# An order planner that looks 3.5 channel tiles ahead instead of 2.5, and fills 0.9 of TensorE's pauses instead of 0.8

## The chip, the cores and the metric

The kernel runs on one core of a Trainium2 chip. A time is the device time of one execution in microseconds (us). One core has TensorE (PE in the profile, with PEld for its weight loads), VectorE (DVE), ScalarE (ACT), GpSimd (POOL) and SyncE (SP, which here only issues DMAs). Each engine runs its own instructions in the order in which the program holds them, and waits on semaphores for the others.

## What is computed

The input x is (2, 48, 48, 768) in float32: two sequences of 2304 tokens with 768 channels. Two layers follow each other, both with a group norm ahead and a residual add behind:

```python
x = x + _L0_conv_ref(_gn(x), w_qkv, w_out)      # 7x7 neighbourhood attention, 12 heads of 64
x = x + _L1_conv_ref(_gn(x), in_proj_w, ...)    # a bidirectional selective scan
```

The second layer is the longer one. It projects the tokens to 1536 inner channels x and as many gates z, and for each direction (forwards with one set of weights, backwards with another):

```python
x = silu(dwconv(x))                              # depthwise, 4 taps
dt, B, C = split(x_proj_w @ x)                   # 48, 16 and 16 rows
delta = softplus(dt_proj_w @ dt + dt_proj_b)
h[t] = exp(delta[t] * A) * h[t-1] + (delta[t] * x[t]) * B[t]     # 16 states for each channel
y[t] = sum over states (h[t] * C[t]) + x[t] * D
```

The result is `out_proj_w @ ((y_forward + y_backward) * silu(z))`.

## The kernel before

**Units.** The scans are cut into 288 units: 2 sequences, 2 directions, 6 chunks of 384 tokens, 12 tiles of 128 channels. `scan` (L1180) writes down one unit, which has number x. It has four groups of four states (`group`, L1211), and each group has these steps:

- the fill of an `hb` tile with delta * x * B, 128 x 1544 (`first`, L1225), on DVE or on POOL; the plan may choose for three of the four groups (`alt`)
- four exponentials on ACT into a `da` tile in PSUM (L1247); there are two `da` tiles, and each holds what one scan instruction takes
- two scan instructions on DVE (L1258), each for two states
- the product with C on POOL (L1273), and a copy of the last state on ACT (L1281)
- twelve transposes on PE that add the group's products into `py` (`add_up`, L1290)

There are seven `hb` tiles; one is free again when its `add_up` is done. Behind the four groups ACT copies `py` to `yt` (L1316). Forwards it goes to memory; backwards PE turns back and adds both directions (L1343), DVE multiplies by the gate (L1353), and the result goes to memory. For three units at a time `deltas_of` (L1128) loads x, makes the products for delta on PE (L1151), the softplus on ACT (L1162, with a table load before and behind it) and delta * x on POOL (L1175).

**Jobs.** All else is work beside the scans: the projections of attention with its scores, softmax and outputs (`attention`, L529), the projection to x and z with the convolution taps on DVE (`in_proj`, L880; taps at L935), the projection to dt, B and C (`x_proj`, L1048) and the output projection (`out_proj`, L1057). Matrix products go through `product` (L372, matmuls at L382), three matmuls to a piece. For sequence 0, attention stands alone ahead of the scans; for sequence 1 it stands beside the scans of sequence 0.

**The plan.** Nothing of this is issued at once. Every piece of work is added to an `Order` (L91) with its engine, an estimated duration, the cells that it reads and writes, and a key. The key is a due time counted in units: 17.25 means a quarter into unit 17. Work flagged `job` fills in; all other work is a main. `Order.run` (L153) then walks through a model of the five engines and sets the order:

- `mains` holds the keys of the mains that are not placed yet. The lowest is `mains[-1]`. Only work with a key up to `horizon`, which is that key plus `LOOK` (L170), may be placed. If nothing can be placed, the horizon is moved by 1 until something can.
- For each engine it takes the piece with the best rank: the earliest start first, where all that could start within 150 ns count as equal, and then the lowest key. `early` lowers the key in this comparison: by 20 for delta's steps, by 4 for `add_up`.
- A piece waits where its buffer tag is still full (`BUFS`, L314: 5 for weights `w`, 7 for `hb`, 2 for `u`, `dlt` and `uz`, 2 for the PSUM banks `mm`).
- A piece ahead of the lowest main that would hold up an exponential is set back by half of that (L193).

Where the model sees PE without work for over 800 ns inside a unit, it puts idle transposes there (`idle`, L1487): matmuls on the identity that go to unused columns of `py` (L1491). Their number is a share of the pause less 300 ns, divided by 109 ns.

```python
gap = t - free["PE"]
if e == "PE" and spare and gap > self.GAP:
    y = Work()
    y.eng, y.ns, y.key, y.job, y.size = e, 0.8 * (gap - 300.0), x.key, True, 0
```

The order that comes out is the program. The estimated durations set nothing but this order.

Of the kernel before, what the change touches and what calls it, by code (L numbers as in the profile page):

```python
# [93 lines left out]
class Order:  # L94
# [2 lines left out]


    SEM = 90.0
    LOOK = 2.5  # L100
    DUE = 100.0
    GAP = 800.0
    TAIL = {"PE": 120.0, "ACT": 50.0, "DVE": 45.0, "POOL": 10.0, "SP": 0.0}
# [49 lines left out]
    def run(self):  # L153
        free = dict.fromkeys(self.TAIL, 0.0)
        ready = {e: [] for e in free}
        slots, dma = {}, 0.0
        mains = sorted((x.key for x in self.works if not x.job), reverse=True)
        done_keys = {}
        for x in self.works:
            if not x.waits:  # L160
                ready[x.eng].append(x)
                assert not x.alt
        out = []
        left = len(self.works)
        extra, spare = 0.0, False
        while left:
            while mains and done_keys.get(mains[-1], 0):
                done_keys[mains[-1]] -= 1
                mains.pop()
            horizon = (mains[-1] if mains else 1e9) + self.LOOK + extra  # L170
            best = None
            for e, works in ready.items():
                pick = None
                soon = min((max(free[e], x.ready) for x in works if x.due), default=1e12)
                for x in works:
                    if x.key > horizon:
                        continue
                    t, more = max(free[e], x.ready), {}
                    for b in x.bufs:
                        if not b.end:  # L180
                            had = slots.get((b.pool, b.tag), ())
                            n = more[b.tag] = more.get(b.tag, 0) + 1
                            if len(had) + n > b.bufs:
                                old = had[n - 1 - b.bufs]
                                if old.left:
                                    t = None
                                    break
                                t = max(t, old.end + self.SEM)
                    if t is None:
                        continue  # L190
                    over = 0.0
                    if mains and x.key > mains[-1] < self.last and not x.due:
                        over = max(0.0, t + x.ns - soon - self.DUE) / 2  # L193
                    rank = (max(t + over, free[e] + 150.0), x.first)
                    if pick is None or rank < pick[0]:
                        pick = rank, t, x
                if pick and (best is None or pick[1] < best[0]):
                    best = pick[1], pick[2], e
            if not best:

                extra += 1.0
                assert extra < 400, "the plan is stuck"
                continue
            extra = 0.0
            t, x, e = best
            ready[x.eng].remove(x)
            gap = t - free["PE"]
            if e == "PE" and spare and gap > self.GAP:
                y = Work()
                y.eng, y.ns, y.key, y.job, y.size = e, 0.8 * (gap - 300.0), x.key, True, 0  # L210
                y.then, y.bufs, y.due, y.fn = [], [], False, lambda y=y: self.idle(y.ns)
                out.append((free[e], y))
            if x.opens is not None:
                spare = x.opens
            if x.alt:
                ready[x.alt[0]].remove(x)
                if e != x.eng:
                    x.eng, x.ns = x.alt
            for b in x.bufs:
                if not b.end:  # L220
                    slots.setdefault((b.pool, b.tag), []).append(b)
            free[x.eng] = t + x.ns
            if x.eng == "SP":
                dma = max(dma, t + 500.0) + x.size / 290.0
                end = max(dma, t + x.ns) + 2100.0
            else:
                end = t + x.ns + x.tail
            for b in x.bufs:
                b.left -= 1
                b.end = max(b.end, end)  # L230
            for y in x.then:
                y.waits -= 1
                y.ready = max(y.ready, end + self.SEM * (y.eng != x.eng))
                if not y.waits:
                    ready[y.eng].append(y)
                    if y.alt:
                        ready[y.alt[0]].append(y)
            if not x.job:
                done_keys[x.key] = done_keys.get(x.key, 0) + 1
            out.append((t, x))  # L240
            left -= 1
        return out
# [1299 lines left out]
```

## Time and profile before

| | |
|---|---|
| median of 4 runs | 7051.0 us (7042.06 to 7054.28) |
| the profiled execution | 7042.06 us, of which 7040.3 us are the span from the first instruction to the last |
| mean granted TensorE clock in it | 0.977 |
| busy in the span | DVE 6062.6 us, PE 6318.4, POOL 5447.4, ACT 4971.3 |
| first scan, end of the last scan | 1053 us, 7003.6 us |
| scan instructions (L1258) | 2304, 1749 ns each |
| idle transposes (L1491) | 4431 in 324 pauses |

Busy time of PE counts a matmul from its start to its modelled end, and overlapping ones once. An arrow `<-` in a wait names what ended it. The clock is the share of full speed that the throttle granted to TensorE. In the lines of waits the three numbers are the total in us, the number of waits, and the longest.

Five stages follow from what stands beside the scans: attention of sequence 0 alone (0 to 1053 us), scans with input projections of sequence 0 (to about 2060 us), scans nearly alone (to 2460 us), scans with the attention of sequence 1 and then the start of its input projections (to 4260 us), and scans with the projections of sequence 1 and all output projections (to the end).

### The profile page before, as it was taken

How to read it: one execution, taken by the hardware profiler on the slowest of the kernel's cores; microseconds unless marked ns; L12 is line 12 of the kernel's file. 1: busy time of each engine (PE TensorE's matmuls, PEld its weight loads, DVE VectorE, ACT ScalarE, POOL GpSimd, SP SyncE). 2: the span in 40 equal slices, each digit the busy share in tenths (PEclk: the TensorE clock that was granted, in tenths of full speed). 3: DMA queues.
4: the chain of work that ended last, by engine and by line, in shares of the span. 5: the costliest groups of instructions: out<-in, count | busy, mean ns of one | idle time of the engine just before them, and what ended most of it. 6: DMA issues, size and time to landing. Idle time of an engine off the chain costs nothing.

```text
span 7040.3 us, 105645 instructions
## 1 busy us (share of the span) xinstructions
PE 6318.4 (90%) x38151; PEld 4831.2 (69%) x38151; DVE 6062.6 (86%) x6217; ACT 4971.3 (71%) x10948; POOL 5447.4 (77%) x1951
## 2 busy tenths in 40 slices
PE   7999989999989998999988888888888898999888
PEld 5666556666666776676666656666678887777777
DVE  2353449999999999998998999999999999999998
ACT  1332248788888788887888778788876667777764
POOL 0000008888989999898898878999999999999997
PEclk9999989999999999999999999999999999999999
DMA  6565454445556444554444354343466676655553
GB/s 190 172 203 173 139 163 126 135 142 153 155 157 197 151 148 140 152 175 148 127 144 133 112 168 135 97 143 113 140 181 189 179 217 194 194 178 156 161 171 104
DMA packets 1337699, 1101.32 MB, mean 156 GB/s; under 512 B 136329, under 2 KB 1327417, under 8 KB 1337145
## 3 DMA queue, kind: packets, MB, share of 16 engines
q1 hardware_dynamic: 1337176, 1094.56, 51.9%
q8 instruction: 303, 4.96, 0.3%
q14 instruction: 220, 1.79, 0.1%
HBM read 881.41 MB, written 213.57 MB: 156 GB/s over the span
## 4 chain that ended last, share of the span: by engine, by line
DVE 39%; PE 18%; ACT 16%; POOL 12%; issue 9%; DMA 5%; SPq 1%; DVEq 0%; POOLq 0%; ACTq 0%
DVE hb L1258 26%; POOL hb L1273 8%; DVE hb L1225 7%; ACT da L1247 5%; PE mm_qk L382 4%; POOL hb L1225 4%; DVE uz_u L935 4%; PE mm_ao L382 2%; PE mm_v L382 2%; PE py L1290 2%; PE mm_xin L382 2%; ACT pr L785 1%; DMA bc<-xdb 1%; ACT pT L832 1%; ACT L1163 1%
## 5 line engine op out<-in xcount | busy, mean ns | idle before, releaser
L1258 DVE TENSOR_TENSOR_SCAN hb<-da,hb 128x772 f32<-128x772 f32 x2304 | 3927.9, 1749 | 179.4 <-ACT da L1247 144.8
L1273 POOL TENSOR_TENSOR hb<-hb,bc 128x1536 f32<-128x1536 f32 x1152 | 3654.0, 3187 | 371.7 <-DVE hb L1258 332.7
L1247 ACT ACTIVATE da<-dlt,A 128x384 f32<-128x384 f32 x4608 | 2677.2, 584 | 916.4 <-DVE hb L1258 845.0
L1290 PE MATMUL py<-ident,hb 128*128 128x128 f32 x13824 | 1747.9, 279 | 267.6 <-POOL hb L1273 260.3
L1290 PEld LDWEIGHTS py<-ident,hb 128*128 128x128 f32 x13824 | 1563.6, 143 | 526.2 <-POOL hb L1273 420.6
L1225 POOL TENSOR_TENSOR hb<-u,bc 128x1544 f32<-128x1544 f32 x495 | 1584.6, 3203 | 22.0 <-PE py L1290 15.3
L1225 DVE TENSOR_TENSOR hb<-du,bc 128x1544 f32<-128x1544 f32 x657 | 1143.4, 1746 | 36.2 <-ACT du L1202 26.2
L1175 POOL TENSOR_TENSOR u<-dlt,u 128x384 f32<-128x384 f32 x288 | 263.8, 918 | 531.8 <-ACT dlt L1162 418.4
L382 PE MATMUL mm_z<-xc,w_z 128*128 128x384 f32 x1728 | 608.7, 492 | 6.9 <-ACT dlt L1157 3.8
L382 PE MATMUL mm_xin<-xc,w_x 128*128 128x390 f32 x1656 | 591.0, 502 | 26.4 <-DVE uz_u L935 16.7
L382 PE MATMUL mm_out<-stage_y,w_o 128*128 128x192 f32 x3168 | 560.5, 332 | 17.9 <-ACT dlt L1157 6.4
L1491 PE MATMUL py<-ident 128*128 128x128 f32 x4431 | 551.2, 277 | 0.0
L382 PEld LDWEIGHTS mm_out<-stage_y,w_o 128*128 128x128 f32 x3168 | 521.5, 193 | 29.4 <-ACT dlt L1157 10.6
L1491 PEld LDWEIGHTS py<-ident 128*128 128x128 f32 x4431 | 504.6, 143 | 28.8 <-issue 25.9
L901 POOL MEMSET xc<- 128x18 f32 x4 | 0.5, 123 | 633.8 <-DVE sm L779 633.8
L382 PEld LDWEIGHTS mm_xin<-xc,w_x 128*128 128x128 f32 x1656 | 310.5, 195 | 239.2 <-issue 36.2
L935 DVE SCALAR_TENSOR_TENSOR uz_u<-mm_xin,conv_w,uz_u 128x384 f32<-128x384 f32 x792 | 428.7, 610 | 49.9 <-ACT uz_u L928 47.7
L382 PE MATMUL mm_qk<-xc_xn,w_qk 128*128 128x384 f32 x1296 | 458.6, 500 | 14.3 <-DVE ev L601 2.6
L382 PEld LDWEIGHTS mm_z<-xc,w_z 128*128 128x128 f32 x1728 | 314.4, 192 | 193.4 <-issue 8.8
L382 PEld LDWEIGHTS mm_qk<-xc_xn,w_qk 128*128 128x128 f32 x1296 | 240.4, 194 | 173.7 <-issue 21.0
L785 ACT ACTIVATE pr<-pr,sm 128x308 f32<-128x308 f32 x432 | 234.5, 544 | 126.1 <-DVE sm L779 126.0
L1306 PE MATMUL py<-ident,vt 128*128 128x128 f32 x864 | 155.4, 290 | 150.8 <-ACT yt L1316 150.4
(163 smaller groups left out, 6768.5 us busy)
## 6 DMA issues: line engine op xcount, KB each, us to landing
w_o<-in_w_opT SPq DMA_DIRECT2D x264, 384.0 KB
bc<-xdf SPq DMA_DIRECT2D x96, 768.0 KB
bc<-xdb SPq DMA_DIRECT2D x96, 768.0 KB
w_qk<-in_w_qkv SPq DMA_DIRECT2D x144, 384.0 KB
w_x<-in_w_inT SPq DMA_DIRECT2D x144, 384.0 KB
w_z<-in_w_inT SPq DMA_DIRECT2D x144, 384.0 KB
w_ao<-in_w_out SPq DMA_DIRECT2D x72, 384.0 KB
u<-uf SPq DMA_DIRECT2D x48, 576.0 KB
```

Of the source, the lines that this page charges most:

```text
L382: nc.tensor.matmul(acc[:m, o0 : o0 + cl], wb[:, wi, wo : wo + m], xb[:, xi, xo : xo + cl], start=c == 0, stop=c == n - 1,)
L785: nc.scalar.activation(pr[j].ap, pr[j].ap, AF.Exp, bias=sm[:, j : j + 1], scale=-1.0, accum_out=sm[:, 2 + j : 3 + j],)
L832: copy(pT[:nk, ks, j, :], bank(pt, 512 - P)[:nk, ks.start * P : ks.stop * P].rearrange("p (k q) -> p k q", q=P),)
L935: nc.vector.scalar_tensor_tensor(u, px[:, at[j] : at[j] + cl], q["conv_w"][:, k, j : j + 1], u, ALU.mult, ALU.add,)
L1175: lambda j=j: nc.gpsimd.tensor_mul(u[:, j, h], dl[:, j, c], u[:, j, h]), at + 0.06 + 0.25 * j,
L1225: on.tensor_mul(cells(hb, SG), by.unsqueeze(1).to_broadcast([P, SG, W]), bc[g].ap)
L1247: lambda: nc.scalar.activation(cells(da, 2)[:, j % 2, h], dl[:, jd, c], AF.Exp, scale=q["A"][:, k, i : i + 1]),
L1258: lambda: nc.vector.tensor_tensor_scan(flip(hb[at2]), flip(da[:, : 2 * W]), flip(hb[at2]), 0.0, ALU.mult, ALU.add),
L1273: lambda: nc.gpsimd.tensor_mul(cells(hb, SG)[:, :, h], cells(hb, SG)[:, :, h], bc[NSG + g][:, :, c]),
L1290: nc.tensor.matmul(py[:tp, t * P : (t + 1) * P], cells(hb, SG)[:, j, h][:, tb[t]], ident, start=False, stop=g == NSG - 1 and j == SG - 1 a ...
L1306: nc.tensor.matmul(py[:tp, t * P : (t + 1) * P], vt[:, tb[t]], ident, start=t == 0, stop=False, is_transpose=True, skip_group_check=True,)
L1491: nc.tensor.matmul(marks["py"][:, CL : CL + P], ident, ident, start=False, stop=False, is_transpose=True, skip_group_check=True,)
```

## The change

```diff
-    LOOK = 2.5
+    LOOK = 3.5
```

```diff
             if e == "PE" and spare and gap > self.GAP:
                 y = Work()
-                y.eng, y.ns, y.key, y.job, y.size = e, 0.8 * (gap - 300.0), x.key, True, 0
+                y.eng, y.ns, y.key, y.job, y.size = e, 0.9 * (gap - 300.0), x.key, True, 0
```

The first edit lets work be placed whose key is up to 3.5 units past the lowest unplaced main. The second makes the idle transposes of a pause take up 0.9 of the pause less 300 ns. All instructions but the idle transposes are the same ones as before; what moves is their order on every engine, and for some fills (L1225) whether DVE or POOL does them.

## The prediction, made before the changed kernel ran

> **What bounds the kernel now.** I read the page first: busy shares and slices.
>
> ```profile
> PE 6318.4 (90%) x38151; PEld 4831.2 (69%) x38151; DVE 6062.6 (86%) x6217; ACT 4971.3 (71%) x10948; POOL 5447.4 (77%) x1951
> ...
> PE   7999989999989998999988888888888898999888
> ...
> DVE  2353449999999999998998999999999999999998
> ```
>
> PE looks busiest over the whole span, but the slices part it: in the first six (to 1053 us) PE is full and DVE at 0.2 to 0.5, then DVE is at 0.9 to the end. PE's later busy time also holds the idle transposes. The chain of work that ended last agrees:
>
> ```profile
> DVE 39%; PE 18%; ACT 16%; POOL 12%; issue 9%; DMA 5%; SPq 1%; DVEq 0%; POOLq 0%; ACTq 0%
> ```
>
> DVE leads, but with ACT, PE and POOL between: DVE stops for each of them. The busy time by stage says how much it stops.
>
> ```profile
> 0.00:1060.00 1060.00, 971.24 (x5063) 640.67 (x5064) 426.26 (x1512) 315.95 (x849) 13.33 (x17) 0.97 0.58 174
> 1060.00:2060.00 1000.00, 910.49 (x4810) 656.15 (x4809) 927.68 (x794) 819.23 (x1565) 876.66 (x314) 0.97 0.47 143
> 2060.00:2460.00 400.00, 370.75 (x2189) 284.06 (x2188) 386.48 (x240) 310.66 (x669) 382.89 (x138) 0.99 0.60 177
> 2460.00:4260.00 1800.00, 1616.98 (x10506) 1202.62 (x10505) 1657.67 (x1716) 1469.25 (x3620) 1559.08 (x554) 0.98 0.48 146
> 4260.00:6660.00 2400.00, 2116.29 (x13406) 1764.79 (x13404) 2329.82 (x1721) 1825.07 (x3782) 2294.21 (x820) 0.98 0.55 163
> 6660.00:7040.00 380.00, 332.63 (x2186) 282.93 (x2185) 334.72 (x240) 231.14 (x466) 321.20 (x113) 0.99 0.46 135
> ```
>
> After the window come PE, PEld, DVE, ACT, POOL, the clock, the DMA share and GB/s. DVE's idle time is 72 us in the second stage, 14 in the third, 142 in the fourth (attention beside scans), 70 in the fifth, 45 at the end: 343 us of 5980. DVE's own work hardly changes, so those 343 us are all that a new order can win from, or add to. The waits of DVE in the fourth stage say on whom:
>
> ```profile
> DVE hb L1258 <- ACT da L1247: 62.2, 54, 5.5
> DVE zs L1353 <- PE mm_yb L1343: 23.4, 10, 4.3
> DVE pr L779 <- PE mm_s L769: 16.3, 10, 5.8
> DVE hb L1225 <- PE py L1290: 8.7, 4, 4.2
> ```
>
> By far the most is the scan that waits for its exponentials; then come waits on PE, 52 us with the smaller ones (2.3 and 1.3 us). The same view gives 69.6 us on ACT and none on PE in the second stage, 11 on ACT in the third, 39 on ACT and 5.6 on PE in the fifth.
>
> **What the change does to the order.** I compared the order of instructions of both programs, engine by engine.
>
> - Until the first scan every engine has the same instructions placed: on PE 432 matmuls for q and k, 432 for v, 216 for attention's output, 72 for x. Attention pieces stand a few places apart; the weights for v are now fetched ahead of most of those for q and k. That load falls into the time in which PE waits for the group norm (28 to 44 us), so I cost it at nothing; bounds -6 and +6 us, the time that 1.18 MB take at the 190 GB/s of the page's first slice.
> - From the last unit's scans to the end the products stand in the same order. The 37 us behind the last scan stay.
> - In between, attention of sequence 1 runs up to 2 to 4 units earlier (608 masked-score instructions placed on DVE at unit 102 instead of 584), and its next input projection is 30 taps ahead at unit 144. In the second stage the jobs are where they were or later (168 taps instead of 180 at unit 12): there the horizon isn't what holds them, but the buffers.
> - DVE gets 659 fills instead of 657, POOL two fewer. PE gets 5127 idle transposes instead of 4431.
>
> **The sum, term by term, against the profiled execution (7042.06 us).**
>
> *Fills.* From the groups:
>
> ```profile
> L1225 POOL TENSOR_TENSOR hb<-u,bc 128x1544 f32<-128x1544 f32 x495 | 1584.6, 3203 | 22.0 <-PE py L1290 15.3
> L1225 DVE TENSOR_TENSOR hb<-du,bc 128x1544 f32<-128x1544 f32 x657 | 1143.4, 1746 | 36.2 <-ACT du L1202 26.2
> ```
>
> Two more on the engine that sets the end: 2 x 1.746 = +3.5 us. POOL's 6.4 us less lie beside.
>
> *Waits on PE.* A job that stands between two `add_up`s holds back the release of `hb` and `py`. I laid the rows of PE's order out with durations from the trace (24 matmuls of 384 columns in 7.94 us, so 0.33 us each; 0.115 for 128 columns, 0.165 for 192, 0.11 for a transpose; idle ones left out), and summed, between each two `add_up`s, what goes over 5 us; seven `hb` tiles cover less. In the fourth stage this falls from 76.9 to 56.3 us, by 27%, and stretches over 10 us go from eight to four. 27% of the 52 us of waits is -14 us. In the second it rises from 1.4 to 6.5 us and in the fifth from 0.3 to 4.2: there waits on PE are 0 and 5.6 us now, so little is known. Bounds 0 and +9 us; I take 0, since the stretches there mostly stay under 6 us.
>
> *Waits on ACT.* A scan waits if ACT's order holds more work between two exponential pairs than DVE's order holds between the scans two apart (two `da` tiles). With the mean durations of the groups, the excess summed over 2304 scans is 745 us before and 730 after; the trace has 215 us of real waits on ACT, so such a sum is only good as a ratio. By stage: second 153.9 to 171.1 (+11% of 69.6 us: +8, of which I take half, as two `da` tiles' lead can hide it), third 42.7 to 35.4 (-17% of 11: -2), fourth 287.5 to 265.4 (-8% of 78: -6), fifth level (0), end 16.9 to 14.9 (-1). Together -5 us; bounds -9 and +8.
>
> *Idle transposes.* 696 more at 109 ns (their pitch in the timeline) are 76 us in 325 pauses, 0.23 us each. After the old ones PE still stood idle for 0.45 us in the median pause, which hides the rest; in 105 pauses under 0.06 us was left, and there the next `add_up` or product starts up to 0.23 us later: at most 105 x 0.23 = +25 us if all were on the path. On the other side the clock: 0.97 to 0.99 in the scan stages. At 1.00, 2% of the some 300 us that PE has on the chain behind the first stage (18% of 7040 less 971) would be -6. I take 0: most of these pauses end at `add_up`, with `hb` tiles in hand.
>
> Do transposes keep the clock up at all? Near the end (6860 to 6990 us) `add_up` and idle transposes are 72 of PE's 112 busy us, and the granted clock there is 1.00, so the row says they do, and the term keeps both its ends. The Trainium skill (TensorE: Matmul & The Clock Gate, Part 4: PE-mode transpose) says the opposite, that transposes don't count as busy for the clock gate; by it the second edit could only cost, and the sum below would lie between itself and 25 us more.
>
> Sum: +3.5 - 14 - 5 + 0 = -15.5, so 7026.5 us for an execution like the profiled one. That was the fastest of the four runs, 9 us under their median, so **7036 us** as a median: -0.2%.
>
> **The rivals.**
>
> *It cancels, or the look binds little.* Against the gain stands that most of DVE's waiting is on the `da` ring, and no horizon widens that:
>
> ```profile
> ACT da L1247 <- DVE hb L1258: 845.0, 1239, 3.8
> ```
>
> ACT stands ready for 845 us and waits for a scan to free a `da` tile: the exponentials are already as far ahead as two tiles let them. The Trainium skill (Perfetto Trace Analysis, Identifying Performance Opportunities) reads a gap that repeats on the engine that should be full as too few buffers for the next tile; by it the look would give nothing, and the sum would be the fills' +3.5 alone, 7054 us in the scale of the median. By the rows: if the fourth stage's relief is halved (-10 instead of -20) and the second stage takes its +8: 3.5 - 10 - 3 + 8 = -1.5, so 7050 us in the scale of the median. Counting anything from 7037 to 7065 (the 0.2% that a measurement of this kernel can tell from no change): 0.26.
>
> *Slower: jobs in front of `add_up`.* A longer look offers PE more jobs whose inputs are there, and each that starts just before an `add_up` is ready holds it. In the order, stretches of over 4 us between `add_up`s rise from 15 to 23 in the second stage, from 33 to 38 in the fourth, from 14 to 19 in the fifth: 18 more. A DVE wait of this kind costs 2.3 us now (23.4 us in 10 waits). If all hit: +42, with the fills and the second stage's ACT waits +53.5, so 7104; if two thirds hit and the fourth stage gains nothing, +28 + 11.5, so 7090. It decides as soon as 13 of the 18 hit while the fourth stage's relief stays: 13 x 2.3 = 30 cancels the 15.5 and the 14 us of the bound. For it: the second and fifth stages have low waits on PE now and only lose. Against it: seven `hb` tiles have covered most stretches under 6 us so far. Chance of slower by over 0.2%: 0.32; likeliest time in that case 7085.
>
> *The forecast*, where the fourth stage's relief holds: 0.42.
>
> **Numbers.** Range: down to 6995, where all 52 us of PE waits in the fourth stage go (38 more than I took, and 3 more on ACT); up to 7100, near the far end of the slower rival. I leave about 0.08 below and 0.1 above.
>
> **What would show it.** Right: first scan at 1053 us within 6; DVE's idle time from 2460 to 4260 us down from 142 to about 122, with fewer waits for mm_yb and mm_s; 659 fills on DVE; idle in the second stage near 72 to 80 us. For the slower rival: waits of L1353, L1079 or L1225 on PE in the second and fifth stages, where there were 5.6 us. For cancelling: 343 us of DVE idle behind the first scan, only elsewhere. Wrong altogether: a DMA wait that neither program's order shows, or a first stage that moves by over 10 us.

## The result, and the profile after

The changed kernel takes 7055.5 us (median of 33 runs, 7040.7 to 7070.46) against 7048.2 us for the kernel before on the same chip (median of 53 runs, 7033.77 to 7070.19). The ratio is 1.001, 95% interval 1.0005 to 1.0015: slower by 0.1%, where 0.2% faster was forecast. The forecast's range holds the time, its sign is wrong.

The profiled execution of after took 7063.15 us (span 7061.4, mean granted clock 0.978), 8 us over its median; that of before took 7042.06, 6 us under its own. Of the 21 us between the two traces only 7 us lie between the medians, which has to be kept in mind below.

The page's busy line of after, and the engines' shares of its chain:

```profile
PE 6400.2 (91%) x38847; PEld 4898.2 (69%) x38847; DVE 6071.5 (86%) x6219; ACT 4977.9 (70%) x10948; POOL 5443.2 (77%) x1949
...
DVE 42%; PE 22%; ACT 16%; issue 9%; POOL 7%; DMA 4%; SPq 0%; DVEq 0%; POOLq 0%; ACTq 0%
```

The two fills that went to DVE are there (6219 instructions instead of 6217), and PE has 696 matmuls and 82 us more. Next the busy times of after by stage, in the same stretches and columns as in the prediction:

```profile
0.00:1060.00 1060.00, 985.34 (x5145) 646.83 (x5146) 439.46 (x1520) 332.05 (x873) 20.32 (x20) 0.98 0.58 174
1060.00:2060.00 1000.00, 909.17 (x4772) 651.25 (x4772) 922.43 (x789) 813.05 (x1559) 887.24 (x316) 0.97 0.48 144
2060.00:2460.00 400.00, 372.41 (x2170) 282.33 (x2168) 388.36 (x246) 313.31 (x675) 375.88 (x136) 0.99 0.57 171
2460.00:4260.00 1800.00, 1621.87 (x10579) 1218.21 (x10578) 1646.19 (x1709) 1452.71 (x3583) 1541.74 (x548) 0.97 0.48 146
4260.00:6660.00 2400.00, 2152.17 (x13824) 1794.71 (x13823) 2314.58 (x1701) 1814.89 (x3754) 2275.71 (x813) 0.98 0.55 160
```

The stretches are fixed in time and the work isn't: in the first, DVE is busy for 13 us more, because the scans begin earlier. So from here on I count the span in parts: the time until the first scan starts, DVE's busy time from there on, and DVE's idle time from there on. Only about 3 us behind the last DVE instruction are left over. The fill alone (first of the experiments below) has before's order but for the idle transposes, so it stands here as a second execution of that order:

| profiled execution | first scan starts, us | DVE busy behind it | DVE idle behind it | span |
|---|---|---|---|---|
| before | 1053.0 | 5641.0 | 343.4 | 7040.3 |
| the fill alone | 1050.3 | 5641.2 | 344.6 | 7039.0 |
| after | 1040.5 | 5649.7 | 367.8 | 7061.4 |
| after less before | -12.5 | +8.7 | +24.4 | +21.1 |

Two effects of opposite sign: the first stage got 12 us shorter (10 against the fill alone), and the scans stop for 24 us more. By stage, second to last, with the stages cut at the same scans in every run, DVE's idle time is 79, 11, 157, 86 and 35 us, where it was 75, 13, 142, 70 and 43 (69, 15, 151, 70 and 40 with the fill alone: a single stage can differ by 8 us between two executions of one order). The fourth stage, for which I had forecast the gain, lost 15 us (6 against the fill alone), and the fifth 16. DVE's waits of after in 2460 to 4260 us (total, number, longest) say where in the fourth:

```profile
DVE hb L1258 <- ACT da L1247: 67.4, 59, 6.2
DVE zs L1353 <- PE mm_yb L1343: 17.4, 9, 5.7
DVE sm L800 <- ACT pr L785: 14.7, 11, 5.2
DVE pr L779 <- PE mm_s L769: 10.6, 7, 5.1
DVE uz_u L935 <- ACT uz_u L928: 10.3, 11, 2.7
DVE xr_x L705 <- PE mm_ao L382: 7.8, 3, 3.8
DVE hb L1225 <- PE py L1290: 6.4, 5, 4.6
```

Waits for `mm_yb` and `mm_s` did fall, from 39.7 to 28.0 us, but `mm_ao` gave some back (1.3 to 7.8). Everything on ACT rose: the scans' exponentials by 5 us, the softmax by 7 (7.8 to 14.7), the taps by 8 (2.7 to 10.3). Together ACT's part is 100 us instead of 78 (81 with the fill alone).

How such a wait looks is shown by the largest new one, in the fifth stage (DVE's idle time in the units from 168 on rose from 5 to 22 us in twelve units, and it did so again in the run with the look alone). From the timeline of after (start, duration, engine, line; in brackets the idle time before and what ended it):

```profile
4766.97 1.28 ACT L961 ACT_TABLE_LOAD   x1
...
4768.27 2.13 ACT L961 ACTIVATE uz_u<-uz_u 128x2304 f32<-128x2304 f32 x1
...
4770.24 5.11 PE L382 MATMUL mm_xin<-xc,w_x 128*128 128x390 f32 x12
4770.41 1.28 ACT L962 ACT_TABLE_LOAD   x1
...
4775.39 1.23 ACT L928 ACTIVATE uz_u<-mm_xin,conv_b,conv_w 128x384 f32<-128x384 f32 x2 [2.50 <-PE mm_xin L382]
4776.52 0.58 ACT L1247 ACTIVATE da<-dlt,A 128x384 f32<-128x384 f32 x1
4776.66 3.24 DVE L935 SCALAR_TENSOR_TENSOR uz_u<-mm_xin,conv_w,uz_u 128x384 f32<-128x384 f32 x6 [6.25 <-ACT uz_u L928]
```

ACT has a SiLU with its two table loads (4.7 us from 4766.97), then a few short copies, then stands for 2.5 us at L928 for the projection's matmuls, and the exponentials of the next scan are queued behind L928. DVE waits 6.25 us at a tap. What ends this wait is PE's product (5.11 us from 4770.24), and L928 directly behind it; the SiLU had ended 3.7 us earlier and isn't on this path. So a wait that the profile puts down to ACT is here in large part one for PE. Nothing in it is a new instruction. It is the same pieces laid in another order, and here a product on PE, its copy on ACT and the tap on DVE fell together.

### The profile page after: what moved, and what is told of

It reads as the page before. It is cut to its first block, busy times and chain, and to the rows that moved or that the text cites. A ratio compares the mean times of both kernels' runs of the same rounds, so it can differ in the third digit from the quotient of the medians.

```text
span 7061.4 us, 107020 instructions
## 1 busy us (share of the span) xinstructions
PE 6400.2 (91%) x38847; PEld 4898.2 (69%) x38847; DVE 6071.5 (86%) x6219; ACT 4977.9 (70%) x10948; POOL 5443.2 (77%) x1949
## 3 DMA queue, kind: packets, MB, share of 16 engines
q1 hardware_dynamic: 1337176, 1094.56, 51.8%
## 4 chain that ended last, share of the span: by engine, by line
DVE 42%; PE 22%; ACT 16%; issue 9%; POOL 7%; DMA 4%; SPq 0%; DVEq 0%; POOLq 0%; ACTq 0%
DVE hb L1258 28%; DVE hb L1225 7%; POOL hb L1273 5%; ACT da L1247 4%; PE mm_qk L382 4%; DVE uz_u L935 4%; PE mm_v L382 2%; PE mm_ao L382 2%; PE py L1290 2%; POOL hb L1225 2%; PE mm_xin L382 2%; PE da L825 1%; ACT uz_u L928 1%; ACT pr L785 1%; PE mm_z L382 1%
## 5 line engine op out<-in xcount | busy, mean ns | idle before, releaser
L1225 POOL TENSOR_TENSOR hb<-u,bc 128x1544 f32<-128x1544 f32 x493 | 1578.7, 3204 | 41.1 <-PE py L1290 30.6
L1225 DVE TENSOR_TENSOR hb<-du,bc 128x1544 f32<-128x1544 f32 x659 | 1146.6, 1747 | 41.8 <-ACT du L1202 29.8
L1491 PE MATMUL py<-ident 128*128 128x128 f32 x5127 | 625.7, 276 | 0.0
L1491 PEld LDWEIGHTS py<-ident 128*128 128x128 f32 x5127 | 577.9, 142 | 32.5 <-issue 29.3
L382 PEld LDWEIGHTS mm_z<-xc,w_z 128*128 128x128 f32 x1728 | 315.9, 192 | 196.9 <-issue 12.5
L1151 PE MATMUL mm_dl<-dt,dtw 49*128 49x384 f32 x576 | 250.3, 538 | 53.3 <-ACT dlt L1157 18.6
```

The source lines that it names most:

```text
L382: nc.tensor.matmul(acc[:m, o0 : o0 + cl], wb[:, wi, wo : wo + m], xb[:, xi, xo : xo + cl], start=c == 0, stop=c == n - 1,)
L1151: lambda j=j, acc=acc: nc.tensor.matmul(acc[:, c], w[:, j * P : (j + 1) * P], dt[:, c], start=True, stop=True),
L1225: on.tensor_mul(cells(hb, SG), by.unsqueeze(1).to_broadcast([P, SG, W]), bc[g].ap)
L1491: nc.tensor.matmul(marks["py"][:, CL : CL + P], ident, ident, start=False, stop=False, is_transpose=True, skip_group_check=True,)
```

## The experiments

Two theories stood against each other. **A: the fill costs nothing, and the look's new order is what moved the time; it is one deal of the pieces among many**, whose stops can't be read from PE's or ACT's order alone. **B: either the fill lengthens PE's work, or looking further ahead has a cost of its own**, with more pieces in front of those that are due. A deal is here any order that the plan lays from the same pieces. The letters in the expectations are each run's own. Each kernel ran beside the kernel before on one chip (7 to 12 executions, 4 of the runs without idle transposes and with late jobs set back), and each ratio is to that one; it can differ by up to 0.05% from the quotient of the two medians. "Idle" is DVE's idle time behind the first scan in the profiled execution; before has 343.4 us.

**The fill alone**

```diff
-                y.eng, y.ns, y.key, y.job, y.size = e, 0.8 * (gap - 300.0), x.key, True, 0
+                y.eng, y.ns, y.key, y.job, y.size = e, 0.9 * (gap - 300.0), x.key, True, 0
```

> The second edit alone: look 2.5, pauses filled to 0.9. The plan's model doesn't count the idle transposes, so every other instruction keeps its place, and only the number of idle transposes rises (about 4431 x 9/8). Theory A (a re-dealt order made the 7 us): level with before, within 4 us, first scan and DVE's idle time unchanged. Theory B (the fill runs over and delays the adds): 5 to 10 us slower, with more waits of DVE on PE. Theory C (a higher clock): 3 to 6 us faster, with a granted clock above 0.977.

Measured: 7046.55 us against 7046.19, ratio 0.9998 (0.9989 to 1.0007). First scan at 1050.3 us, idle 344.6. The order is the one of before but for the idle transposes, and the sum of the stops is the same. A holds: the second edit does nothing that could be told from zero within 0.1%.

**The look alone**

```diff
-    LOOK = 2.5
+    LOOK = 3.5
```

> The first edit alone: look 3.5, pauses filled to 0.8. The order is that of the changed kernel, with fewer idle transposes. Theory A (the re-dealt order makes the difference): 5 to 10 us slower than before, as the whole change. Theory B (the fill makes it): level with before within 4 us.

Measured: 7056.59 us, ratio 1.0015 (1.0006 to 1.0024). First scan at 1039.5, idle 361.6: by stage 75, 9, 160, 83 and 35 us, nearly what after has. From before to here the parts are -13.5, +5.2 and +18.2 us, together +10, which is the ratio. The whole effect of the change is the first edit's.

**No idle transposes at all**

```diff
-                y.eng, y.ns, y.key, y.job, y.size = e, 0.8 * (gap - 300.0), x.key, True, 0
+                y.eng, y.ns, y.key, y.job, y.size = e, 0.0 * (gap - 300.0), x.key, True, 0
```

> Look 2.5 and no idle transposes at all; every other instruction keeps its place. It prices the whole fill. If the fill is free and only holds the clock: a lower granted clock (0.90 or less in the scan stages) and 5 to 40 us more. If the transposes do nothing for the clock: the clock stays at 0.977 and the time stays within 5 us, or falls by up to 25 us where they ran into the adds.

Measured: 7116.61 us, ratio 1.0105 (1.0091 to 1.0119). In the profiled execution (7134.48 us, the longest of the four) the mean granted clock is 0.932 instead of 0.977, the first scan starts at 1061.2, idle is 419.6. Three of its stretches:

```profile
1060.00:2060.00 1000.00, 843.88 (x3930) 580.22 (x3928) 923.01 (x794) 808.57 (x1547) 875.89 (x311) 0.92 0.46 140
...
2460.00:4260.00 1800.00, 1549.21 (x9512) 1141.48 (x9511) 1632.05 (x1683) 1439.43 (x3567) 1539.20 (x546) 0.94 0.46 141
4260.00:6660.00 2400.00, 1963.12 (x11140) 1589.62 (x11138) 2294.41 (x1709) 1805.90 (x3713) 2247.20 (x802) 0.91 0.55 162
```

The clock is the seventh column, 0.91 to 0.94 where before had 0.97 to 0.98. So the idle transposes do hold the clock, and they are worth 1% in all. The clock fell less than expected (0.90 or less), and the time rose more (5 to 40 us). From 0.8 to 0.9 nothing of that is left to win: the clock of the fill alone is 0.980.

**A constant that means nothing: 91 ns instead of 90 for a release in the plan's model**

```diff
-    SEM = 90.0
+    SEM = 91.0
```

> A control: look 2.5, fill 0.8, and the plan's allowance for a semaphore 91 ns in place of 90. It means nothing by itself, but ties fall otherwise and most of the order is dealt anew. Theory A (any new deal moves the time by some 5 to 25 us either way): a difference from before of 5 us or more, of either sign, with DVE's idle time behind the first scan moved by as much. Theory B (only a longer look moves the time): level within 4 us.

Measured: 7055.16 us, ratio 1.0014 (1.0005 to 1.0023); idle 357.7, of it 154 in the fourth stage, where waits on ACT are 103 us. This is a control: 1 ns in a model that only sets the order. It costs as much time as the look does. The fourth stage's idle time alone would not show it (151 with the fill alone), but its waits on ACT do, 103 us against 78 and 81, and after has 100.

**The same constant at 89**

```diff
-    SEM = 90.0
+    SEM = 89.0
```

> A second control: look 2.5, fill 0.8, and 89 ns for a semaphore in the plan in place of 90. Theory A (before is one deal among many, and a lucky one for its neighbours): 0 to 15 us slower, as with 91. If before is an ordinary deal: equally likely faster or slower, by 5 to 15 us.

Measured: 7042.27 us, ratio 0.9991 (0.9982 to 0.9999). Idle is 353.6, 10 us more than before, but this deal leaves 650 fills to DVE instead of 657, and DVE's busy time is 12 us less. The expectation that before is a lucky deal, with 0 to 15 us to lose, missed: this one is some 6 us faster.

**The longer look only while the lowest due time is before -3, that is in the first stage**

```diff
-            horizon = (mains[-1] if mains else 1e9) + self.LOOK + extra
+            look = 3.5 if mains and mains[-1] < -3.0 else self.LOOK
+            horizon = (mains[-1] if mains else 1e9) + look + extra
```

> Look 3.5 only until the lowest unplaced due time reaches -3 (attention of sequence 0), 2.5 behind it, fill 0.8. The order of the scans is nearly that of before. In the runs so far the order with look 3.5 had its first scan at 1040 us and that with 2.5 at 1050 to 1054. Theory A (the first stage wins some 12 us, the scans lose some 20): 8 to 14 us faster than before, first scan at about 1041 us, DVE idle for 343 us behind it as before. Theory B (the early first scan is paid back in the scans, for instance because later work isn't there yet): level with before, and more than 350 us idle behind the first scan.

Measured: 7033.74 us, ratio 0.998 (0.9971 to 0.9989). First scan at 1040.8, idle 348.8; the fourth stage's is 142, as before. The first stage's 12 us can be had alone. This version is the fastest of all, by 0.2% against before; its margin over the 0.14% that a meaningless 1 ns moved is small, and it rests on one deal.

**Late jobs are set back as well.** The model sets a piece back that would hold up an exponential, but not a job that is itself overdue. If such jobs on ACT make the waits, this should take them away:

```diff
-                    if mains and x.key > mains[-1] < self.last and not x.due:
+                    if mains and (x.job or x.key > mains[-1]) and mains[-1] < self.last and not x.due:
```

> Look 2.5, fill 0.8, and the setback of work that would hold up an exponential holds for jobs that are late too, so that six norms no longer stand in a row on ACT. Theory A (DVE waits where ACT holds a long block of job work between exponentials): DVE's waits on ACT fall from 215 us to 190 or less, and the time by 10 to 30 us. Theory B (the blocks are no cause, any deal gives about this): within 10 us of before, waits on ACT at 205 to 225 us.

Measured: 7143.99 us, ratio 1.0134 (1.0121 to 1.0147), idle 459.6. Neither expectation came. The waits of DVE in the fourth stage:

```profile
DVE uz_u L935 <- ACT uz_u L928: 70.6, 16, 15.0
DVE hb L1258 <- ACT da L1247: 47.4, 44, 4.2
DVE pr L779 <- PE mm_s L769: 18.1, 10, 11.7
DVE xr_x L705 <- PE mm_ao L382: 15.7, 7, 3.6
DVE ev L601 <- PE mm_qk L382: 10.9, 4, 6.6
```

The wait aimed at fell (62.2 to 47.4 us), and the one for the jobs themselves rose from 2.7 to 70.6: a tap or a score stands in DVE's order too, and if its input is set back on ACT, DVE stops there instead, with the scans queued behind it. The order that favours the exponentials did not remove the waits on ACT; it moved them.

**Looks of 3.0 and 2.0**

```diff
-    LOOK = 2.5
+    LOOK = 3.0
```

> Look 3.0, fill 0.8. If the length of the look has an effect of its own on the scans, this lies between 2.5 (0) and 3.5 (+10 us): about +5. If each length is just another deal: anywhere from -10 to +20 us, with the first scan somewhere between 1040 and 1054 us.

Measured: 7062.06 us, ratio 1.0015 (1.0006 to 1.0023); first scan 1054.7, idle 367.7.

```diff
-    LOOK = 2.5
+    LOOK = 2.0
```

> Look 2.0, fill 0.8. If the scans' idle time grows with the length of the look, this has less than 343 us of it and is 5 to 15 us faster behind the first scan. If each length is a deal, it has 340 to 380 us. In either case the first scan at 1050 us or later.

Measured: 7072.21 us against 7055.65, ratio 1.0022 (1.0014 to 1.0031); first scan 1050.4, idle 364.7, 660 fills on DVE. A shorter look costs more than the longer one does: time doesn't rise with the look.

**The longer look with the other two deals**

```diff
-    SEM = 90.0
-    LOOK = 2.5
+    SEM = 89.0
+    LOOK = 3.5
```

> Look 3.5, fill 0.8, and 89 ns for a semaphore in the plan in place of 90: the longer look dealt anew. With look 2.5 the deals 90, 89 and 91 gave 343, 354 and 358 us of DVE idle behind the first scan; with 3.5 the deal 90 gave 363 and 370. Theory A (only the deal counts): 340 to 360 us idle here, first scan near 1040 us, 5 to 15 us faster than before. Theory B (the longer look costs the scans some 20 us by itself): 365 us or more, 5 us or more slower than before.

Measured: 7080.31 us, ratio 1.0031 (1.002 to 1.0043); first scan 1040.0, idle 392.9, 184 of it in the fourth stage. Its waits there:

```profile
DVE hb L1258 <- ACT da L1247: 76.4, 64, 6.7
DVE zs L1353 <- PE mm_yb L1343: 19.9, 8, 5.3
DVE hb L1225 <- PE py L1290: 19.3, 7, 10.7
DVE xr_x L705 <- PE mm_ao L382: 18.3, 8, 8.8
DVE pr L779 <- PE mm_s L769: 10.8, 7, 5.1
```

```diff
-    SEM = 90.0
-    LOOK = 2.5
+    SEM = 91.0
+    LOOK = 3.5
```

> Look 3.5, fill 0.8, 91 ns for a semaphore: the same question with another deal. Theory A: 340 to 360 us of DVE idle behind the first scan, 5 to 15 us faster than before. Theory B: 365 us or more, 5 us or more slower.

Measured: 7052.27 us, ratio 0.999 (0.9981 to 0.9999); first scan 1049.3, idle 353.6. By their expectations the deal at 89 ns speaks for a cost of the look itself and the one at 91 ns against it. So one nanosecond up or down makes the longer look's kernel 0.1% faster or 0.3% slower than before. The ratios by look:

| look | model's release 89 ns | 90 ns | 91 ns |
|---|---|---|---|
| 2.0 | | 1.0022 | |
| 2.5 | 0.9991 | 1 (before) | 1.0014 |
| 3.0 | | 1.0015 | |
| 3.5 | 1.0031 | 1.0015 | 0.999 |

At 2.5 the mean is 1.0002, at 3.5 it is 1.0012. Each has a spread of 0.2 to 0.4% over deals that mean nothing, and the neighbours on both sides of 2.5 are slower than it. Before is also the deal with the least idle time behind the first scan of all that ran (343 us; the others have 345 to 460).

**One load of the group norm earlier**

```diff
-            ("SP", 400, fetch, [mv], [gT]),
+            ("SP", 400, fetch, [gs], [gT]),
```

> Look 2.5, fill 0.8; the group norm's second small load (w_gTb) is planned behind the first one instead of behind the statistics, so that on SP's queue it stands ahead of the fetch of xc. The order of the scans changes in a few places only. Theory A (that queue order is the larger part of the first stage's 12 us): PE's wait for w_gTb falls from 4.8 to 1 us or less, the first scan comes at 1044 to 1048 us, 4 to 8 us faster. Theory B (the 12 us come from attention itself): first scan at 1049 us or later, within 3 us of before.

This looks for the 12 us of the first stage. In before's timeline, between attention of sequence 0 and its group norm:

```profile
938.84 0.56 DVE L705 TENSOR_TENSOR xr_x<-mm_ao,xr_x 128x384 f32<-128x384 f32 x1 [2.72 <-PE mm_ao L382]
939.80 0.43 SPq L889 DMA_DIRECT2D xc<-x1T  x1
940.32 0.58 SPq L431 DMA_DIRECT2D w_gTb<-c_gmatT  x1
946.22 2.69 PE L457 MATMUL mm_gnb<-gn_gb,w_gTb 32*128 32x1 f32 x12 [4.81 <-DMA w_gTb<-c_gmatT]
```

and in after's:

```profile
916.37 0.84 SPq L889 DMA_DIRECT2D xc<-x1T  x1
...
935.24 0.38 SPq L431 DMA_DIRECT2D w_gTb<-c_gmatT  x1
937.54 1.47 PE L457 MATMUL mm_gnb<-gn_gb,w_gTb 32*128 32x1 f32 x12 [0.77 <-DMA w_gTb<-c_gmatT]
```

In before the load of the group matrix (96 KB) is issued right behind the fetch of `xc` (1161 KB), on the same DMA queue. By the packets of the trace the fetch's data move from 940.9 to 945.0 us and the load's only from 944.5 on, and PE waits 4.8 us for it. In after the fetch was issued at 916.37, 19 us ahead of the load, and the queue is free of it by then: the load's packets move from 936.3 to 936.9. PE's wait for this load is 0.8 to 1.0 us in all runs with a look of 3.0 or 3.5, and 4.8 to 5.4 us in those that keep 2.5 and the load's old place. With the edit above, which plans the load earlier in every group norm, the wait is gone at a look of 2.5 too, and from the last `mm_ao` to the first scan it takes 108 us instead of 114 (113 with the fill alone; after: 106). But attention ended at 942.0 instead of 938.8 us in this deal, so the first scan came at 1050.1 and not where A had put it. Ratio 0.9988 (0.9979 to 0.9997), idle 361.4, with 653 fills on DVE. So the queue accounts for some 5 of the 12 us. The other part is the end of attention itself, 934.2 in after, and 936.5 to 944.6 in the other deals of looks from 2.0 to 3.0, but for the one with late jobs set back (934.9). It isn't the look's for sure: with 91 ns and a look of 3.5 attention ended at 942.9, and that deal's first scan is at 1049.3.

## Why the prediction was wrong

**The idle transposes: right.** Taken as 0 in bounds of -6 and +25. Alone they gave 0.9998; the 82 us more of PE work lie in PE's pauses, and the clock rose from 0.977 to no more than 0.980. That transposes keep the clock up was read from one stretch; taking them away showed it (0.932 and 1.05%). The sentence of the Trainium skill that was weighed there (TensorE: Matmul & The Clock Gate, Part 4: PE-mode transpose) doesn't hold for these float32 transposes, which are issued as transposes (`is_transpose=True`).

**The fills: right.** 659 instead of 657 on DVE. DVE's busy time behind the first scan grew by 5.2 us with the look alone, 3.9 of them at L1225.

**The first stage: wrong.** Taken as 0 within 6 us, and it moved by 12.5 (13.5 with the look alone). I weighed the early load of v's weights, and compared the places of PE's matmuls, which were the same. What I did not compare were SP's places: a small load that had been queued right behind a fetch of 1161 KB. In after that fetch went out 19 us ahead of the load. By the prediction's own words this was "wrong altogether", and some 5 us of it are the one gain of the look with a known cause.

**The waits on PE: sized too large, by a misread price.** In the fourth stage -14 was forecast and -6.5 came (51.8 to 45.3; -3.3 with the look alone; and 56.8 with the fill alone, so the change is hardly clear of what one order gives twice). The price was half of the true one. The sum took 0.33 us for each matmul of 384 columns that the program has, but 24 matmuls in 7.94 us is a count of the trace's records, and the trace shows two records for each of these products: up to the first scan the program has 432 matmuls for q and k, and the trace 864 (number, then nanoseconds of one, then first and last start in us).

```profile
L382 PE MATMUL mm_qk<-xc_xn,w_qk x432: 486/486/1009, 44.0 to 603.8; 128*128 128x384 f32 x144
...
L382 PE MATMUL mm_qk<-uz_xn,w_qk x432: 486/486/591, 115.3 to 756.2; 128*128 128x384 f32 x144
```

With every record counted, PE's sum for the fourth stage falls from 294 to 276 us, by 6% and not by 27%, which would have made the term -3 us. Stretches over 4 us then rise from 52 to 54 in the second stage, 83 to 87 in the fourth and 87 to 88 in the fifth, 7 and not 18 more. The fifth stage gave back 8 us (4 with the look alone), at the far end of the bound that I gave for the second and the fifth.

**The waits on ACT: the step that failed.** "-6" for the fourth stage came as +22 (77.7 to 100.3; 99.3 with the look alone; 81.3 with the fill alone), and "level" for the fifth as +11 (39.2 to 50.4). Behind the first scan they went from 205 to 239 us in all, +34 (+29 with the look alone), where -5 was forecast. The step took a sum over ACT's order against DVE's order as a ratio of real waits, and did the same for PE. Laid out in the same way for the other orders, the two sums for the fourth stage say nothing of the waits that the trace then has (the columns are the look, and the model's release where it isn't 90 ns; 3.5 is the run with the look alone; the stage is cut at the same scans in all, which for 3.5 gives 263 where the prediction had 265.4; PE's sums are at the prediction's price):

| fourth stage, us | 2.5 (before) | 2.5, 91 | 2.5, 89 | 3.0 | 2.0 | 3.5 | 3.5, 89 | 3.5, 91 |
|---|---|---|---|---|---|---|---|---|
| ACT's sum by the order | 287 | 223 | 285 | 243 | 227 | 263 | 275 | 271 |
| waits on ACT in the trace | 78 | 103 | 84 | 86 | 93 | 99 | 100 | 79 |
| PE's sum by the order | 77 | 68 | 57 | 59 | 64 | 56 | 46 | 71 |
| waits on PE in the trace | 52 | 43 | 51 | 48 | 49 | 48 | 70 | 57 |

The order with the lowest sum for ACT has the longest waits on ACT, and the one with the lowest for PE the longest on PE; over the eight, both pairs rather run against each other. At two records for a product PE's sums are 294, 266, 259, 264, 287, 276, 252 and 285, and 252 still stands with the longest waits. The sum holds each engine against DVE alone, and the stops shown above are made by three: DVE waits for ACT at a tap, ACT waits for PE's product, and the exponentials are queued behind. It also leaves out jobs that DVE itself waits for (softmax and taps, 15 of the 22 us). Why the longer look's orders make ACT stop more stays open. I had one pair of sums and no second order to test them on, and 223 us would have read as a larger gain than the one I forecast.

**The rivals.** Slower by jobs in front of `add_up`: not so. Waits on PE went from 5.6 to 14 us in the fifth stage and stayed under 1 us in the second, against the 13 of 18 waits of 2.3 us that it needed. The rival of cancelling has the right number: 7055.5 lies in its 7037 to 7065. Its reason doesn't fit: the look didn't bind little, it gave 12 us in one place and took 18 to 24 in others. And the 845 us weighed there are ACT's, while the sentence of the Trainium skill cited with them (Perfetto Trace Analysis, Identifying Performance Opportunities) is about the engine that should be full, which here is DVE.

**Shown, and not shown.** Shown: the fill does nothing within 0.1%, the look's order does it all, its two parts have opposite signs, and a change of the plan that means nothing moves the time by about as much in either direction. Only argued: that the loss is the luck of one deal. Three deals of each look have means 0.1% apart with a spread of 0.2% and 0.4%; a cost of the longer look of 0.1% or so could hide in that. What makes one deal stop less than another isn't settled either: the one cause that was tried, overdue jobs on ACT, made it worse when it was treated.

## What to carry to other kernels

Where a planner with buffers and due times sets the order, any edit to its constants deals the whole order anew, so first change a constant that means nothing and see how far the time goes: here 0.14% up and 0.09% down for 1 ns, and up to 0.3% with the longer look. An effect smaller than that belongs to the deal and not to the idea, unless the same stage shows it over several deals. Split the result by stage before giving an edit up: here 12 us could be kept by using the longer look only where it won them. And a sum over an order is a forecast only after it has told known orders apart, and its prices and its counts have to come from the same list, the program's or the trace's.

## What the runs showed of the hardware

The idle transposes, whose product is never used, are worth 70 us between the medians (7116.61 and 7046.19): without them the granted clock falls from 0.977 to 0.932, and in the profiled execution DVE stands idle for 76 us more. Most of that shows up as waits on ACT, not on PE. Behind the first scan the wait of the scans for exponentials grows from 144.8 to 194.8 us (108 to 147 waits), the one of the fills for the copy at L1202 from 16.7 to 29.4, while those of L1353, L779 and L1225 for `mm_yb`, `mm_s` and `py` stay within 2 us. ACT's own waits on PE rose in the same time; before, and then without idle transposes:

```profile
ACT yt L1316 <- PE py L1290: 54.1, 51, 7.6
...
ACT dlt L1157 <- PE mm_dl L1151: 31.7, 43, 3.4
...
ACT dlt L1157 <- PE mm_dl L1151: 72.1, 80, 4.7
ACT yt L1316 <- PE py L1290: 69.4, 64, 7.6
```

By these rows a slower PE reaches the scans mostly through the engine between them.

One program's executions lie 0.5% apart (before: 7033.77 to 7070.19), so a profiled pair may show 21 us where the medians show 7; the parts by stage are safer read from two executions of one order, as here before and the fill alone, and after and the look alone.
